# A graph layer by sorted windows: table copies issued by ScalarE at steps of the sort, and one chunk more in every turn

## The chip, the cores and the metric

The kernel runs on one core of a Trainium2 chip. The metric is the device time of one execution in microseconds, the median of several runs. The engines are named as in the profile: PE (TensorE products), PEld (its weight loads), DVE (VectorE), ACT (ScalarE), POOL (GpSimd) and SP (SyncE, which only issues transfers). A name with q, such as SPq, is the queue side of that engine.

## The reference

For 100,000 nodes of 64 features and 3,300,000 edges, sorted by target node, the layer normalises the features, applies a ReLU, sends the source row along every edge, averages over the edges of a target, and adds the result to the input:

```python
def _L0_gnn_ref(features, src, tgt, W, b):
    num_v = features.shape[0]
    local = features[tgt]
    nbr = features[src]
    x = jnp.concatenate([local, nbr - local], axis=-1)
    y = jnp.einsum('ec,oc->eo', x, W) + b
    s = jax.ops.segment_sum(y, tgt, num_segments=num_v)
    cnt = jax.ops.segment_sum(jnp.ones((y.shape[0],), y.dtype), tgt, num_segments=num_v)
    cnt = cnt[:, None]
    return jnp.where(cnt > 0, s / jnp.maximum(cnt, 1.0), 0.0)

h = jnp.maximum(_layernorm(x, axis=-1), 0.0)
x = x + _L0_gnn_ref(h, src, dst, L0_gnn_W, L0_gnn_b)
```

As the sum is linear, the kernel sums only the rows `h[src]` per target and counts them; the weights are applied once per node at the end.

## The kernel before

The program has five stages, which run one after another in time, with some overlap.

**Rows** (0 to about 440 us). For 28 groups of nodes the kernel normalises `x` and writes every row of `h`, split into three bf16 parts and a column of ones, to a DRAM tensor `h3` (named `h` in the profile; the write is L289, `h<-parts`). A row is 194 bf16 numbers, 388 bytes. It also writes `hb` from ACT's queue and clears the sums `acc`.

**The edges are divided** in two. 120 windows of 16,256 edges (`src_w`, `dst_w`) take the way of sorting; the rest, 377 chunks of 128 x 28 edges (`src_p`, `dst_p`), take the way of gathering.

**Chunks** (the generator `chunks`). For each of the 28 columns of a chunk POOL gathers 128 rows of `h` by an indirect transfer (L388, `nb<-h,si`, five buffers `nb`). DVE makes one-hot rows of the targets (L339, `hot`), PE multiplies them with the gathered rows (L393, `ps<-nb,hot`), DVE adds the three parts (L403, L405, `sums`), and POOL adds `sums` to `acc` by a transfer with accumulation (L365 in the first stages, L370 in the loop), issued 56 gathers after the sums. Index blocks `si` and `di` for 16 chunks are loaded by SP.

**Sort** (about 490 to 2750 us; the generator `sort_windows`). The target column `keys` is loaded (L418), the smallest target of every window found (L420, L422), sixteen pieces `s` of the source column are loaded (L434) and merged into the keys (L437 to L443), and then DVE and ACT run a sorting network. One exchange is an ACT copy `tmp` (L449) and DVE's minimum and maximum (L450, L451). After every step the generator yields its estimated nanoseconds. The caller spends them on gathers, `GATHER` nanoseconds for one:

```python
def gathers(ns):
    nonlocal owed
    owed += ns
    while owed > 0:
        next(ev, None)
        owed -= GATHER
```

At every second step from the 40th on the caller also writes one copy of 640 rows of `h` into the DRAM tensor `tables` (L891, 157 copies of 242.5 KB), in the layout in which the later stages load them. A scheduler then decides the order on each engine's queue: an instruction is placed as early as its priority and the modelled readiness of its inputs allow, unless `tc.issue_after(x)` sets it behind the instruction `x`. `last` holds, for each engine, the last instruction that others may be set behind.

**Filling of slots** (about 2750 to 3510 us; `fill_slots`). POOL fetches pieces of the sorted keys (322 gathers `kf<-ksort`, L692, and 120 gathers `kx<-ksort`, L663); DVE, ACT and PE turn them into index tables in DRAM.

**Pairs and turns** (`pairs`). For each pair of windows PE picks rows out of `tables` by one-hot products (L822, `gp<-tab,gh`), ACT moves them (L825, L826) and PE adds them by target (L836, `total<-gs,dh`). The first three pairs partly overlap the filling of slots; 57 more run in a loop of three turns of 19 pairs, with `KB` chunks of the gathering way in each turn. All chunks that are not in a turn are worked off ahead of the loop: `FIRST` and `KB` give their number, `PA`, as chunks in all minus three times `KB`. A closing stage (from about 16,205 us, L995 to L1015) applies the weights and writes the output.

Of the kernel before, what the change touches and what calls it, by code (L numbers as in the profile page):

```python
# [22 lines left out]
POOL = mybir.EngineType.Pool  # L23
SP = mybir.EngineType.SP
DVE = mybir.EngineType.DVE

P = 128
EPS = 1e-5
J = 28
CHUNK = P * J  # L30
SB = 19
KB = 102
U0 = 3
KG = 16
JH = 14
LAG = 3
GATHER = 1230
STEP = 1300
GAP = 8
JA = 16  # L40
# [2 lines left out]
CS = 640  # L43
NB = CS // P
# [15 lines left out]
TG = 3  # L60
# [3 lines left out]
def f32_of(bits):  # L64
    return float(np.array([bits], np.uint32).view(np.float32)[0])
# [12 lines left out]
def plan(v, e):  # L78
# [3 lines left out]
    turns = max(1, min((P // 2 - U0) // SB,  # L82
                       round((e - FIRST * CHUNK - 2 * U0 * ew) / (2 * SB * ew + KB * CHUNK))))
    nw = 2 * (U0 + turns * SB)
    chunks = -(-(e - nw * ew) // CHUNK)
    return wl, nw, max(chunks, turns * KB)


FIRST = 71


@with_exitstack
def gnn_preln(ctx: ExitStack, tc, x, src_w, dst_w, src_p, dst_p, src_a, dst_a, wT, b, out, V, E):
# [17 lines left out]
    nc = tc.nc  # L111
# [19 lines left out]
    NCH = src_p.shape[0]  # L131
    PA = NCH - (SETS - U0) // SB * KB
    NMT = -(-NCH // P)
# [9 lines left out]
    h3 = dram.tile([RT, CT], BF16, name="h3")  # L143
# [9 lines left out]
    tables = dram.tile([NTB, P, TG, NB * CT], BF16, name="tables")  # L153
# [157 lines left out]
    with tc.tile_pool(name="rows", bufs=5) as rows, \  # L311
# [3 lines left out]
        last = {}  # L315
# [5 lines left out]
        def behind():  # L321

            return tc.issue_after(last[DVE].ins) if DVE in last else nullcontext()

# [6 lines left out]
        def add_now(all_of_them=False):  # L331
            while later and (all_of_them or (later[0][0] <= count[0] and count[0] - count[1] >= GAP)):
                later.pop(0)[1]()
                count[1] = count[0]
# [76 lines left out]
        def drain(events):  # L411
            for _ in events:
                pass

        def sort_windows(keys, piece, small, ps):
# [5 lines left out]
            nc.vector.tensor_scalar_min(wb[:, 0:1], wb[:, 0:1], float(V - CH))  # L421
            last[DVE] = nc.vector.tensor_reduce(wb[:, 1:2], whole[:, :EW], axis=AX.X, op=ALU.max)  # L422
            yield 2 * EW
# [6 lines left out]
            for a in range(0, EW, PART):  # L430
# [11 lines left out]
                nc.vector.tensor_scalar(s[:, :n], s[:, :n], 10, BIAS | 1, op0=ALU.logical_shift_left, op1=ALU.bitwise_or)  # L442
                last[DVE] = nc.vector.scalar_tensor_tensor(d, d, 1, s[:, :n],  # L443
                                               op0=ALU.logical_shift_left, op1=ALU.bitwise_or)
# [1 line left out]
            nc.vector.memset(keys[:, EW:], f32_of(END))  # L446

            def exchange(lo, hi, tmp):
                nc.scalar.copy(tmp, lo)  # L449
                nc.vector.tensor_tensor(lo, tmp, hi, ALU.min)  # L450
                last[DVE] = nc.vector.tensor_tensor(hi, tmp, hi, ALU.max)  # L451

            def merge(p, k):
# [3 lines left out]
                def blocks(b, q, m):  # L457
                    r = keys[:, 2 * p * b:2 * p * (b + q)].rearrange("p (b l) -> p b l", l=2 * p)
                    if k < p:
                        r = r[:, :, k:2 * p - k]  # L460
                    r = r.rearrange("p b (m s t) -> p b m s t", s=2, t=k)
                    tmp = ps.tile([NW, PIECE], F32, name="tmp")
                    exchange(r[:, :, :, 0], r[:, :, :, 1],
                             tmp[:, :q * m * k].rearrange("p (b m t) -> p b m t", b=q, t=k))

                def run(a, n):
                    tmp = ps.tile([NW, PIECE], F32, name="tmp")
                    exchange(keys[:, a:a + n], keys[:, a + k:a + k + n], tmp[:, :n])

                def groups(a, n):  # L470
                    r = keys[:, a:a + 2 * k * n].rearrange("p (m s t) -> p m s t", s=2, t=k)
                    tmp = ps.tile([NW, PIECE], F32, name="tmp")
                    exchange(r[:, :, 0], r[:, :, 1], tmp[:, :n * k].rearrange("p (m t) -> p m t", t=k))
# [41 lines left out]
            def around(c):  # L515
                a = min(max(c // 2 * step + c % 2 * (step // 2) - H, 0), WL - L)
                return slice(a, a + L)

            def count_next():
                nonlocal nth  # L520
                nth += 1
                nc.scalar.activation(junk[:, 0], keys[:, around(nth)], AF.Sign, bias=bound[:, nth:nth + 1],
                                     scale=-GAIN, accum_out=pos[:, nth:nth + 1])

            p = 1
            while p < WL:
                k = p
# [37 lines left out]
            lo = piece.tile([NW, NHB + 2], F32, name="lo", bufs=1)  # L565
# [4 lines left out]
            for c in range(here + 1, NHB + 1):  # L570
                if nth < here:
                    count_next()
                last[DVE] = nc.vector.tensor_scalar(junk[:, 1], keys[:, around(c)], f32_of(BIAS + (c * CSH << 10)), None, op0=ALU.is_lt,
                                        op1=ALU.add, accum_out=pos[:, c:c + 1])
# [56 lines left out]
            slots[:] = at_i, first, row, fit, over, limit  # L631
            last.pop(DVE)

# [240 lines left out]
        with tc.tile_pool(name="few", bufs=1) as few:  # L874
            ev = chunks(0, PA)
            owed = 0.0
# [8 lines that stand above are left out]
            with tc.tile_pool(name="keys", bufs=1) as big, tc.tile_pool(name="piece", bufs=2) as piece, \  # L885
                    tc.tile_pool(name="sort_ps", bufs=2, space=PSUM) as ps:
                for i, ns in enumerate(sort_windows(big.tile([NW, WL], F32, name="keys"), piece, few, ps)):

                    k, r = divmod(i - 40, 2)
                    if 0 <= k < NCB and r == 0:  # L890
                        nc.sync.dma_start(tables[k // TG, :, k % TG].rearrange("p (b f) -> p b f", b=NB),  # L891
                                          h3[k * CS:(k + 1) * CS].rearrange("(b p) f -> p b f", b=NB))
                    gathers(ns)
            worst = few.tile([P, 1], F32, name="worst")
            nc.vector.tensor_reduce(worst, odd, axis=AX.X, op=ALU.max)
            with tc.tile_pool(name="w_ps", bufs=1, space=PSUM) as wps:
                w_ps = wps.tile([1, P], F32, name="w_ps")
                nc.tensor.transpose(w_ps, worst, ident)
                w_all = few.tile([1, 1], F32, name="w_all")
                nc.vector.tensor_reduce(w_all, w_ps, axis=AX.X, op=ALU.max)  # L900
                nc.vector.tensor_copy(turns[:, 0:1], w_all)
                nc.vector.tensor_scalar_mul(turns[:, 1:2], w_all, float(NF))

            with tc.tile_pool(name="load", bufs=3) as load, tc.tile_pool(name="hots", bufs=3) as hots, \
                    tc.tile_pool(name="g_ps", bufs=2, space=PSUM) as g_ps, \
                    tc.tile_pool(name="a_ps", bufs=1, space=PSUM) as a_ps:
                with tc.tile_pool(name="slots", bufs=2) as piece:
                    steps = pairs(0, U0, NE - AHEAD // 2)
                    for i, _ in enumerate(fill_slots(piece)):
                        for _ in range(SL // 2 if 2 < i < -(-NS // SL) else 0):  # L910
                            next(steps)
                for _ in steps:
                    gathers(2 * STEP)
                drain(ev)
                add_now(True)
                with tc.For_i(0, (SETS - U0) // SB, 1) as g:
                    ev = chunks(None, KB, PA + g * KB)
                    next(ev)
                    owed = 0.0
                    for _ in pairs(U0 + g * SB, SB):  # L920
                        owed += 2 * (KB * J - 1) / (SB * NE)
                        while owed > 0:
                            next(ev, None)
                            owed -= 1
                    drain(ev)
                    add_now(True)
# [126 lines left out]
```

## Time and profile before

| what | value |
|---|---|
| median of 3 runs | 16530.51 us (16521.81 to 16532.21) |
| the profiled execution, its own time | 16529.2 us |
| its span | 16527.4 us |
| PE busy | 13495.8 us (82%) |
| DVE busy | 13631.9 us (82%) |
| ACT busy | 10590.2 us (64%) |
| POOL busy | 11625.4 us (70%) |
| gathers L388 | 10556, mean 953 ns, 10059.1 us |
| table copies L891 | 157 issues, SP, 365.3 to 861.4 us |

The busy shares are averages over stages with different limits, so they say little by themselves. The timeline and the tables by stretches of time tell which engine is full in which stage. A wait is listed under the engine that waited, with what ended it. "Issue" is idle time that the profile cannot put down to anything. The durations of the program's own DMA issues on POOL are times of POOL, not of the transfer.

### The profile page before, as it was taken

Reading aid. Unit: us, or ns where it says so; the run is one execution under the profiler, and the core shown is the slowest. Engines: PE = TensorE matmul, PEld = TensorE weight load, DVE = VectorE, ACT = ScalarE, POOL = GpSimd, SP = SyncE. Lnnn points to the kernel's source line nnn. Section 1 sums busy time; section 2 is a strip of 40 time slices with the busy share of each in tenths; the row PEclk is TensorE's granted clock in tenths of the full one; section 3 lists DMA queues with packets and bytes.
Section 4 is the critical chain, followed back from the end, with each engine's and each line's share of the span. In section 5 each row is a group of like instructions: output and inputs, shape, how many; then the busy total and the mean of one; then the engine's idle time right before and its main releaser. Section 6 shows DMA issues by size and latency. Waiting matters only on the chain. (4 is left out here: it accounts for less than half of the span.)

```text
span 16527.4 us, 393944 instructions
## 1 busy us (share of the span) xinstructions
PE 13495.8 (82%) x149665; PEld 12959.6 (78%) x149665; DVE 13631.9 (82%) x14528; ACT 10590.2 (64%) x21095; POOL 11625.4 (70%) x11771
## 2 busy tenths in 40 slices
PE   6011110379999999999999999999999999999996
PEld 5011110369999999999899999999989999999996
DVE  6699996468888888888788888888878888888884
ACT  5144335466777777777677777777767777777772
POOL 4577777755777777777677777777767777777765
PEclk7555555689999999999999999999999999999998
DMA  8931112478999989999899999999879999999997
GB/s 295 152 50 39 39 39 63 139 221 255 279 281 280 279 279 279 281 279 278 253 280 279 280 279 279 278 281 278 278 249 279 281 282 280 279 280 279 279 276 282
DMA packets 1769028, 3974.67 MB, mean 240 GB/s; under 512 B 941660, under 2 KB 949607, under 8 KB 1759101
## 3 DMA queue, kind: packets, MB, share of 16 engines
q1 hardware_dynamic: 1289510, 3354.10, 61.8%
q0 software_dynamic: 473424, 569.44, 17.1%
q8 instruction: 1181, 19.35, 0.5%
q10 hardware_dynamic: 4176, 25.74, 0.4%
q14 instruction: 737, 6.04, 0.1%
HBM read 3750.40 MB, written 236.66 MB: 241 GB/s over the span
## 5 line engine op out<-in xcount | busy, mean ns | idle before, releaser
L388 POOL DMA_INDIRECT nb<-h,si x10556 | 10059.1, 953 | 3469.0 <-issue 3083.0
L836 PE MATMUL total<-gs,dh 128*128 128x193 bf16 x77280 | 8067.4, 247 | 65.2 <-ACT whole L844 29.1
L339 DVE TENSOR_TENSOR dh<-dt,c 128x2048 bf16<-128x2048 int16 x4860 | 5893.8, 1213 | 1718.9 <-PE total L836 1660.1
L836 PEld LDWEIGHTS <-dh 128*128 128x128 bf16 x77760 | 6725.8, 97 | 447.3 <-issue 85.1
L825 ACT CAST gs<-gp 64x386 bf16<-64x386 f32 x9420 | 4480.0, 476 | 3506.8 <-PE gp L822 3476.5
L822 PE MATMUL gp<-tab,gh 128*128 128x193 bf16 x56520 | 6356.8, 247 | 251.8 <-DVE gh L796 145.4
L822 PEld LDWEIGHTS <-gh 128*128 128x128 bf16 x58440 | 5092.8, 98 | 275.2 <-DVE gh L796 148.7
L796 DVE TENSOR_TENSOR gh<-srs,c 128x1536 bf16<-128x1536 int16 (+2 forms) x4920 | 4614.7, 939 | 29.1 <-PE gp L822 25.3
L826 ACT CAST gs<-gp 64x386 bf16<-64x386 f32 x9420 | 4494.5, 477 | 109.3
L393 PE MATMUL ps<-nb,hot 128*128 128x193 bf16 x10556 | 1805.6, 264 | 2131.1 <-DVE sums L405 1892.7
L393 PEld LDWEIGHTS <-hot 128*128 128x128 bf16 x10556 | 1044.7, 105 | 2196.3 <-DVE sums L405 1940.6
L449 ACT COPY tmp<-keys 120x1536 f32<-120x1536 f32 (+26 forms) x606 | 750.8, 1248 | 1352.5 <-DVE keys L451 1051.1
L450 DVE TENSOR_TENSOR keys<-tmp,keys 120x1536 f32<-120x1536 f32 (+26 forms) x606 | 867.3, 1466 | 71.2 <-ACT tmp L449 69.8
L451 DVE TENSOR_TENSOR keys<-tmp,keys 120x1536 f32<-120x1536 f32 (+26 forms) x606 | 869.0, 1464 | 1.3
L339 DVE TENSOR_TENSOR hot<-near,c 128x1792 bf16<-128x1792 int16 x754 | 814.2, 1080 | 0.1
L370 POOL DMA_DIRECT2D acc<-sums x306 | 305.9, 1000 | 287.4 <-DVE dh L339 102.4
L855 POOL DMA_DIRECT2D acc<-wsums x120 | 168.4, 1403 | 443.0 <-DVE wsums L851 150.5
L692 POOL DMA_INDIRECT kf<-ksort,at_i x322 | 330.3, 1026 | 110.2 <-issue 93.6
L697 DVE TENSOR_SCALAR sr<-kf 120x768 int32<-120x768 int32 (+1 forms) x27 | 15.3, 568 | 460.4 <-DMA kf<-ksort,at_i 443.5
L828 ACT CAST gs<-gp 128x386 bf16<-128x386 f32 x240 | 115.7, 482 | 203.2 <-PE gp L822 201.5
L1010 ACT COPY catT<-c_ps 128x512 f32<-128x512 f32 x112 | 56.2, 534 | 278.1 <-PE c_ps L1008 278.1
L726 PE MATMUL gp<-ident,df 120*128 120x120 f32 x161 | 30.5, 328 | 247.6 <-ACT df L718 222.5
(169 smaller groups left out, 4101.6 us busy)
## 6 DMA issues: line engine op xcount, KB each, us to landing
tab<-tables SPq DMA_DIRECT2D x3120, 727.5 KB
srs<-sr_d SPq DMA_DIRECT2D x1560, 384.0 KB
nb<-h,si POOLq DMA_INDIRECT x10556
tables<-h SPq DMA_DIRECT2D x157, 242.5 KB
h<-parts SPq DMA_DIRECT2D x28, 1358.0 KB
dt_d<-dt SPq DMA_DIRECT2D x26, 1440.0 KB
dt<-dt_d SPq DMA_DIRECT2D x1560, 24.0 KB
acc<-zeros SPq DMA_DIRECT2D x28, 910.0 KB
```

Of the source, the lines that this page charges most:

```text
L339: nc.vector.tensor_tensor(out.rearrange("p k (a d) -> p k a d", d=D), numbers[:, :, None].to_broadcast(shape), upto[:shape[0], :n].rearran ...
L388: last[POOL] = nc.gpsimd.indirect_dma_start(out=nb[:, j], out_offset=None, in_=h3, in_offset=bass.IndirectOffsetOnAxis(ap=si[:, u, j:j + 1 ...
L393: nc.tensor.matmul(ps, lhsT=before[1][:, j], rhs=before[2][:, j, :CE], start=j == 0, stop=j == J - 1)
L449: nc.scalar.copy(tmp, lo)
L450: nc.vector.tensor_tensor(lo, tmp, hi, ALU.min)
L451: last[DVE] = nc.vector.tensor_tensor(hi, tmp, hi, ALU.max)
L692: last[POOL] = nc.gpsimd.indirect_dma_start(out=kf[:, c, q], out_offset=None, in_=ksort, in_offset=bass.IndirectOffsetOnAxis(ap=at_i[:, c0 ...
L796: nc.vector.tensor_tensor(gh[:, a:z, :, :to].rearrange("p c i b s -> p (c i) b s"), srs[u, s // SL][:, c + a:c + z].rearrange("p c i s -> ...
L822: nc.tensor.matmul(gp[:, i], lhsT=ghots[t][:, i, b], rhs=of[:, :CE], start=b == 0, stop=b == len(parts) - 1)
L825: nc.scalar.copy(gs[t][:KS], gp[:KS])
L826: nc.scalar.copy(gs[t][KS:], gp[KS:, ::-1])
L836: nc.tensor.matmul(total[:, o, b % 2 * CE:b % 2 * CE + CE], lhsT=dhots[t][:, i, b * P:b * P + P], rhs=gs[t][:, i] if s < NS else beyond[u] ...
```

## The change

The copies into `tables` go from SP's queue to ACT's, and each is set behind the ACT copy `tmp` of its step, so that the scheduler cannot move it ahead. Gathers are paced at 1250 ns instead of 1230, every turn gets 103 chunks instead of 102, and `FIRST` goes from 71 to 68, which leaves 68 chunks instead of 71 ahead of the loop. From line 26 on, lines of the changed kernel stand one lower than before, and past L890 two lower.

```diff
+ACT = mybir.EngineType.Activation
...
-KB = 102
+KB = 103
...
-GATHER = 1230
+GATHER = 1250
...
-FIRST = 71
+FIRST = 68
...
             def exchange(lo, hi, tmp):
-                nc.scalar.copy(tmp, lo)
+                last[ACT] = nc.scalar.copy(tmp, lo)
                 nc.vector.tensor_tensor(lo, tmp, hi, ALU.min)
                 last[DVE] = nc.vector.tensor_tensor(hi, tmp, hi, ALU.max)
...
                     k, r = divmod(i - 40, 2)
                     if 0 <= k < NCB and r == 0:
-                        nc.sync.dma_start(tables[k // TG, :, k % TG].rearrange("p (b f) -> p b f", b=NB),
-                                          h3[k * CS:(k + 1) * CS].rearrange("(b p) f -> p b f", b=NB))
+                        with tc.issue_after(last[ACT].ins):
+                            nc.scalar.dma_start(tables[k // TG, :, k % TG].rearrange("p (b f) -> p b f", b=NB),
+                                                h3[k * CS:(k + 1) * CS].rearrange("(b p) f -> p b f", b=NB))
                     gathers(ns)
```

## The prediction

> **What bounds the kernel now.** I read the time in stages, because the page's chain of waits names only the last 1 to 2% (the closing stage, lines L998 to L1015), which the change does not touch. First the slices of the page:
>
> ```profile
> POOL 4577777755777777777677777777767777777765
> DMA  8931112478999989999899999999879999999997
> ```
>
> A slice is 413 us. DMA is busy in the first (rows) and from slice 8 on (turns), idle in the sort between; POOL never drops. The table by stretches shows which engine is full where (PE, PEld, DVE, ACT, POOL busy, clock, DMA share, GB/s):
>
> ```profile
> 600.00:800.00 200.00, 18.12 (x112) 15.45 (x112) 150.37 (x131) 39.12 (x25) 146.00 (x136) 0.53 1.18 149
> 1000.00:1200.00 200.00, 22.29 (x140) 19.49 (x140) 193.81 (x145) 80.37 (x61) 152.17 (x158) 0.53 0.20 41
> 3210.00:3310.00 100.00, 34.87 (x267) 31.47 (x266) 31.09 (x39) 35.34 (x74) 76.84 (x77) 0.65 0.38 119
> 3610.00:3710.00 100.00, 99.79 (x1148) 96.62 (x1146) 85.84 (x90) 72.56 (x153) 68.91 (x71) 1.00 0.88 278
> ```
>
> In the sort (line two) POOL shows 152 of 200 us, but the waits give each gather L388 another 0.30 us of "issue", so 158 instructions fill the 200 us: POOL is full. DVE at 194 is nearly full too. In the filling of slots (line three) only POOL is full. From 3610 on PE is full. The timeline shows that POOL goes from the last gather of the sort straight into the `kf` gathers, with no gap:
>
> ```profile
> 2909.49 0.94 POOL L388 DMA_INDIRECT nb<-h,si  x1 [0.30 <-issue]
> 2910.74 0.99 POOL L692 DMA_INDIRECT kf<-ksort,at_i  x1 [0.31 <-issue]
> ```
>
> DVE had finished its sort at about 2745 us and waits 179 us for these `kf`. So the path is: rows ready, first gather at 489.7, POOL without a pause until the last `kf` at 3510, then PE to 16190, then the closing stage. The start is disturbed. These are waits between 400 and 760 us (engine, line, whom for, total, times, longest) and the gathers' table (PE, POOL):
>
> ```profile
> DVE own L437 <- DMA s<-in_src_w: 85.4, 10, 38.6
> POOL nb L388 <- DMA si<-in_src_p: 48.4, 1, 48.4
> DVE wb L420 <- DMA keys<-in_dst_w: 46.2, 1, 46.2
> ...
> 489.00:880.00 391.00, 37.59 (x224) 264.95 (x255) 0.52 1.16 138
> 880.00:2880.00 2000.00, 227.71 (x1428) 1434.81 (x1514) 0.54 0.20 44
> ```
>
> The 157 table copies L891 leave SP from 365 to 861 us. While they last POOL gathers 255 rows in 391 us, afterwards 1514 in 2000. Subtracting additions L365 (1.626 + 0.30 = 1.93 us; 4 and 54 of them) leaves 1.50 against 1.25 us per gather.
>
> **What the Trainium skill says.** "DMA: Bandwidth & Descriptors", section "Issuing engines are not separate DMA queues": copies from any engine run on the same 16 DMA engines and interleave; another issuer saves only issue time. So moving to ScalarE frees no bandwidth; only the spreading can. This trace cannot test it: nearly nothing leaves ACT. The same page, section "Specifications", puts the smallest transfer for full rate at 512 B. The trace agrees: table rows are 388 B, and copies with gathers move 113 to 166 GB/s at a DMA share above 1.1, where the turns move 280 at 0.9.
>
> **The change, part by part.** I sum against the profiled run (16529.2 us, span 16527.4 plus 1.8); the median of the three runs is 1.3 higher.
>
> (a) Start of the gathers. The order on SP after the change has no copies between the last rows and `keys`. The `h<-parts` pairs left SP at 332.1, 359.9, 387.6, so every 27.8 us; the next, due at 415.4, left at 419.0 behind eight copies (17.68 us of SP). Last `h` therefore goes at about 419 instead of 421.8, last `hb` at 422 instead of 424.3. Landing took up to 9.6 us amid copies (387.64 to 397.24); I take 6, an estimate. `keys` waits for all these: it leaves at 428 instead of 441.6. Its transfer alone moved 195 GB/s (460 to 480 us), so 7.62 MB take 39 us and some 2 us of latency: landed at 469, `si` just behind, first gather at 470 instead of 489.7. **-20 us**; ends -6 (rows land no sooner) and -35 (`keys` at the 270 GB/s of the rows).
>
> (b) Gathers beside copies. 255 x 1.249 + 4 x 1.93 = 326 us against 391: 65 us lost. After the change one copy follows two steps of the sort, about 7 us (two exchanges of two 1.46 us DVE operations, plus one-hots). In the jam 112 copies took 543 to 861 us, 2.8 us each, so copies fill 40% and gathers 0.19 of the DMA engines: 0.6, no jam. In the turns, at 0.9, a gather takes 948 ns (142.21 us for 150 from 8200 to 8400), as in the quiet sort, and the 2856 of a turn wait for their forerunners only 12 us in all. I leave 15 of 65: **-50 us**. Ends: -65 (no loss left) and +11 (all 157 copies cost what the 135 of this stretch did, 0.48 us, so 76).
>
> (c) Pace and split. FIRST 71 to 68 and KB 102 to 103 keep 377 chunks: 68 before the turns instead of 71, 309 in them instead of 306. The instruction order shows 1764 gathers ahead of the first `kf` instead of 1792, and one addition fewer: 28 x 1.249 + 1.93 = **-37 us** on POOL's path (ends -35, -39). I give 1250 no other gain: POOL needs 1.249 plus 1.93/28, so 1.32 us per gather, either way.
>
> (d) PE later. With PE full, 1148 products took 99.79 us, 87 ns each, so a chunk costs 28 x 87 ns = 2.4 us (the 247 ns of the groups are latency). Three more in the turns, +7.3; between last `kf` and turns 10 chunks remain instead of 12, -4.9. **+2 us**; ends 0 and +10.
>
> (e) ScalarE. 157 issues at 0.62 us (two in 1.24 us on SP at 579.06) are 97 us over 314 steps. Behind each stands the next `tmp` copy L449 (after the change L450), for which DVE waits. ACT sits idle before L449 for 1051 us waiting on DVE, so I take 0. If the cover fails, DVE still has room: it starts 20 us earlier and loses the 87 us that it idled between 520 and 720 (113 busy of 200), so its sort ends near 2640 while `kf` starts near 2805. Ends: 0 and SP's median issue, 2.3 us x 157 = 361 us on ACT. A gain is excluded, as ACT gets only work added. SP loses those issues; its index and `s` loads move up. The DMA waits of the ACT copies are on transfers eight issues back, long landed.
>
> (f) POOL in the turns. One chunk more is about 36 us of POOL per turn of some 4065. I counted POOL's gathers minus PE's products in the second turn (from 8060 us): lead 47 after 100 us, 63 after 700, 97 after 2400, then capped by the five `nb` buffers. 28 gathers more over a turn slow that growth from 50 to about 36 per half turn; the lead stays positive. 0 us; ends 0 and +34 per turn.
>
> Sum: -20 - 50 - 37 + 2 = -105. 16529.2 - 105 = 16424, plus 1.3 for the median: 16425 us. `s` loads no longer wait, but that was DVE's time, not POOL's, and adds nothing.
>
> **Rivals.**
> 1. *The copies hinder as before, only spread.* For: POOL's own durations rose beside them (up to 2.7 us). Against: the share of 0.6. Then (b) is +11: -20 + 11 - 37 + 2 = -44, 16487.
> 2. *ScalarE becomes the stall, and it is slower.* Place: ACT's queue between `tmp` copies. If an issue blocks as SP's did (2.3 us), the sort steps slip. An addition is emitted 56 gathers (70 us) after its sums, so POOL absorbs about 70 us of DVE slip and then waits in full. It outweighs the 105 us from 175 us of slip on, 1.1 us per copy; at 2.3 us it gives 361 - 70 - 105 = +186, 16717. For: SP did block. Against: SP blocked behind a full queue, and its unblocked issue is 0.55 to 0.62 us.
> 3. *POOL becomes the bound in the turns.* +34 x 3 = 102 on top: 16527, no change. For: about 190 of 200 us are filled there. Against: the lead that I counted.
> 4. *The copies do not really spread.* Then (c) and (d) remain, -35: 16496. Against: the order shows each behind two `tmp` copies, the first after twelve.
>
> **Chances.** Forecast 0.74, rival 1 0.10, rival 2 0.09, rival 3 0.05, rival 4 0.02. About 0.2% (33 us, below 16497) is what a measurement here can tell from no change. Forecast, 1 and most of 4 are faster: 0.84; rival 3 and the rest of 4 the same, 0.06; rival 2 slower, 0.10. The ends of (a) to (d) without rivals give -139 to -30, 16391 to 16500; I widen down to 16375, since the rows' end may move more than I allow, and cut at 16495.
>
> **What would show it.** Right: first gather near 470; about 1.27 us per gather between 500 and 900; DMA share near 0.6 from 650 to 1800, 0.2 after; first `kf` near 2805, still straight behind a gather; turns unchanged within 5 us each. Wrong: `kf` waiting for DVE or ACT, POOL's additions waiting for `sums`, PE waiting for `nb` inside a turn, or issues of copies on ACT above 1.1 us.

## The result and the profile after

The changed kernel takes **16439.88 us** (median of five runs, 16428.62 to 16441.98), the kernel before took 16531.38 us beside it (median of five). The ratio is 0.9944 with a 95% interval of 0.9929 to 0.9958: 91.5 us less, where 105 were forecast. The profiled execution lasted 16428.62 us, 100.6 us less than the profiled one of before. It is the fastest of the five, 11.3 us under their median, so what is read from the two traces adds up to 100.6 and not to 91.5.

The slices of the page after the change:

```profile
POOL 4677777754777777777677777777767777777775
DMA  7434312488999999998799999999879999999997
```

DMA's 8 and 9 of the first two slices have become 7 and 4, and the fourth and fifth slice have risen from 1 to 4 and 3: the copies have moved out of the first 860 us. The groups of `tables` and the table by stretches (PE, PEld, DVE, ACT, POOL busy, clock, DMA share, GB/s) say where to:

```profile
L893 ACTq DMA_DIRECT2D tables<-h x157: 559/559/691, 686.1 to 1804.2; - x157
```

```profile
470.00:600.00 130.00, 13.28 (x84) 11.49 (x84) 128.70 (x106) 6.19 (x4) 102.63 (x90) 0.53 0.41 85
600.00:686.00 86.00, 13.19 (x56) 6.90 (x56) 82.39 (x65) 29.40 (x19) 66.19 (x66) 0.52 0.20 48
686.00:1804.00 1118.00, 124.55 (x756) 104.48 (x756) 965.93 (x738) 401.52 (x312) 851.11 (x876) 0.54 0.41 74
1804.00:2814.00 1010.00, 114.73 (x729) 99.84 (x729) 912.21 (x970) 499.32 (x641) 768.80 (x792) 0.53 0.22 49
3610.00:3710.00 100.00, 99.50 (x1146) 96.40 (x1144) 87.68 (x101) 71.07 (x150) 71.17 (x73) 1.00 0.88 271
```

The 157 copies leave ACT between 686 and 1804 us, at 0.56 us each. In that stretch DMA is busy to 0.41 and POOL issues 876 instructions, 846 gathers and 30 additions: 846 x 1.249 + 30 x 1.93 = 1114.6 of the 1118 us. Beside the spread copies the gathers lose 3 us in all. The share of DMA alone does not tell whether they lose: from 470 to 600 us, with no copy yet under way, it is 0.41 too, and there the 90 instructions are only 112 us of work in 130 us. With PE full (last line) nothing has changed. The timeline of POOL:

```profile
470.23 1.22 POOL L389 DMA_INDIRECT nb<-h,si  x1 [43.33 <-DMA si<-in_src_p]
...
2812.64 0.95 POOL L389 DMA_INDIRECT nb<-h,si  x1 [0.30 <-issue]
2813.89 0.98 POOL L693 DMA_INDIRECT kf<-ksort,at_i  x1 [0.31 <-issue]
```

The first gather starts 19.5 us earlier, the first `kf` 96.8 us earlier (2910.7 before), and still straight behind a gather. The last `kf` starts at 3404.7 instead of 3509.3, 104.6 earlier. The three turns last 4058.9, 4071.4 and 4072.8 us against 4056.2, 4068.2 and 4071.4, so some 2 us longer each.

Of these waits between 600 and 2900 us (engine, line, whom for; total, times, longest) the two of ACT for DMA were not there before, and the first, of DVE for ACT, came to 69.8 us then, the longest 2.3:

```profile
DVE keys L451 <- ACT tmp L450: 198.1, 79, 122.6
ACT tmp L450 <- DMA si<-in_src_p: 137.6, 2, 127.9
DVE sr L698 <- DMA kf<-ksort,at_i: 95.6, 4, 63.9
ACT tmp L450 <- DMA tables<-h: 67.2, 21, 3.5
```

ACT stood still for 127.9 us in the middle of the sort and DVE behind it for 122.6. DVE waits only 63.9 us for the first `kf` where it waited 179.0 before: the cover of the sort has shrunk to a third, but it held.

On two of the chips of the experiments all engines paused now and then, for tens of us, from about 690 us on, waiting for nothing that the program shows, and the kernel before took 27.1 to 27.3 ms there; runs from there are read only ahead of 690 us or one against another.

### The profile page after: what moved, and what is told of

The parts are those of the page before. It is cut to its first block, busy times and chain, and to the rows that moved or that the text cites. A ratio compares the mean times of both kernels' runs of the same rounds, so it can differ in the third digit from the quotient of the medians.

```text
span 16427.0 us, 393934 instructions
## 1 busy us (share of the span) xinstructions
PE 13503.9 (82%) x149665; PEld 12963.9 (79%) x149665; DVE 13621.6 (83%) x14528; ACT 10590.7 (64%) x21095; POOL 11621.9 (71%) x11771
## 5 line engine op out<-in xcount | busy, mean ns | idle before, releaser
L303 PEld LDWEIGHTS o_ps<-w_own,hT 128*128 128x128 f32 x784 | 155.1, 252 | 79.1 <-ACT hT L298 69.5
```

## The experiments

Every kernel was timed beside the kernel before on the same chip.

**The copies moved, pace and split old** (spread_only, spread_only_b), of the changed kernel:

```diff
-KB = 103
+KB = 102
-GATHER = 1250
+GATHER = 1230
-FIRST = 68
+FIRST = 71
```

> The changed kernel with the old pace and split (GATHER 1230, KB 102, FIRST 71): the copies alone are moved; 64 chunks of gathers stand ahead of the first `kf` as before the change. Theory (POOL's queue sets the first `kf`): the earlier start (-19.5 us) and the contention no longer met (-40 us) remain, the 28 gathers and the addition (-37 us) come back. First gather near 470, first `kf` near 2851, time -60 against before: about 16471 us, all of it ahead of the first `kf`. Rival A (the end of DVE's sort sets the first `kf`, the number of gathers does not): the whole gain stays, about 16440. Rival B (the split and pace carry it all): no gain, about 16531.

> The kernel of spread_only once more, because in its first run the engines paused for tens of us at a time all through the turns, and the kernel before took 27.2 ms there too. The copies alone are moved; pace and split stay old, 64 chunks of gathers ahead of the first `kf`. Theory (POOL's queue sets the first `kf`): -60 us against before, about 16471 us, first gather near 470, first `kf` near 2851 and straight behind a gather. Rival A (the end of DVE's sort sets it): the whole gain stays, about 16440. Rival B (split and pace carry it all): no gain, 16531.

The first run fell on a pausing chip: ratio 0.9987 (0.9980 to 0.9994) at 27220 us, first gather at 473.0. The second took 16464.57 us against 16524.76: ratio 0.9965 (0.9951 to 0.9978), **-60 us** as the theory had it. Its POOL:

```profile
2849.05 0.94 POOL L389 DMA_INDIRECT nb<-h,si  x1 [0.30 <-issue]
2850.30 0.99 POOL L693 DMA_INDIRECT kf<-ksort,at_i  x1 [0.31 <-issue]
```

2850.3 was expected at 2851. The 36.4 us that lie between this and the changed kernel's 2813.9 are one chunk of gathers. DVE's sort had stood still here too (133.6 us on ACT), so the end of the sort sets nothing: rival A is out, and so is B. No run spreads the copies from SP's queue, so whether spreading needs ACT as the issuer is not shown.

**Pace and split new, the copies as before** (split_only, split_only_b), of the kernel before:

```diff
-KB = 102
+KB = 103
-GATHER = 1230
+GATHER = 1250
-FIRST = 71
+FIRST = 68
```

> The kernel before with the new pace and split alone (GATHER 1250, KB 103, FIRST 68), its copies still leaving SP all at once; 63 chunks of gathers ahead of the first `kf`. Theory (POOL's queue sets it): one chunk fewer is 28 x 1.249 + 1.93 = 37 us less ahead of the first `kf`, one more per turn costs PE about 2 us in all: -35, about 16496 us, first `kf` near 2874, still straight behind a gather. Rival A (DVE's sort sets it): DVE is done at about 2745 and unchanged, so nothing is gained, 16531. Rival B (a chunk more in each turn makes POOL the bound there): +34 us in each of three turns, 16530 to 16600, with the turns longer than 4072 us.

> The kernel of split_only once more (the kernel before with GATHER 1250, KB 103, FIRST 68; its copies leave SP all at once), for the reason of spread_only_b; 63 chunks of gathers ahead of the first `kf`. Theory (POOL's queue sets it): 37 us fewer there, some 2 us more of PE in the turns: -35, about 16490 us on this chip, where before took 16525; with the -60 of spread_only_b that makes the whole change. First `kf` near 2874, still straight behind a gather. Rival A (DVE's sort sets it): nothing gained, 16525. Rival B (a chunk more in each turn makes POOL the bound there): 16525 to 16590, with turns longer than 4072 us.

On the pausing chip no difference could be told (1.0000, 0.9992 to 1.0009). The second run took 16535.58 against 16565.89 us: ratio 0.9980 (0.9973 to 0.9988), **-30 us**. `kf` is straight behind a gather again:

```profile
2898.64 0.95 POOL L388 DMA_INDIRECT nb<-h,si  x1 [0.30 <-issue]
2899.89 0.99 POOL L692 DMA_INDIRECT kf<-ksort,at_i  x1 [0.31 <-issue]
```

It comes at 2899.9 and not at 2874. The gathers started at 494.6 instead of 489.7, and 1764 x 1.249 + 57 x 1.93 = 2313 of the 2405 us up to `kf` are work: 92 us lost, where the profile of before lost 71. There is no profile of the kernel before on this chip, whose own time was 35 us longer too, so whether its jam was longer there stays open. The turns last 4060.0, 4072.3 and 4079.3 us, far from 34 us more in each (rival B). The two halves, -60 and -30, make the -91.5 of the whole: they add.

**Twice the copies** (copies_twice, copies_twice_b), of the changed kernel:

```diff
+    spare = dram.tile([NTB, P, TG, NB * CT], BF16, name="spare")
...
-                        with tc.issue_after(last[ACT].ins):
-                            nc.scalar.dma_start(tables[...
+                        for to in (tables, spare):
+                          with tc.issue_after(last[ACT].ins):
+                            nc.scalar.dma_start(to[...
```

> The changed kernel, but ScalarE issues each copy twice, the second into a spare table that nobody reads (extra work, same output). Theory (spread copies fit beside the gathers, the DMA engines have room): share of the DMA engines between 700 and 1800 us rises from about 0.42 to about 0.65, gathers keep 1.25 to 1.29 us each, and the loss is 0 to 15 us; ScalarE's second issue, 157 x 0.56 = 88 us, falls on DVE's sort, which ended near 2752 while the first `kf` is issued at 2814, so up to 26 us of it may show: 16440 to 16480 us. Rival A (each copy takes its price from the gathers, spread or not, 0.26 to 0.48 us as in the jam): another 40 to 76 us on POOL's path between 690 and 1800 us, 16480 to 16515, gathers there at 1.30 us or more. Rival B (issues on ScalarE stall the sort by more than they last): the additions of POOL wait for `sums` or `kf` for DVE, over 16500.

> The kernel of copies_twice once more, for the reason of spread_only_b: the changed kernel, but ScalarE issues each copy twice, the second into a spare table that nobody reads. The changed kernel is taken as 92 us under the kernel before. Theory (spread copies fit beside the gathers): DMA share between 700 and 1800 us from about 0.42 to about 0.66, gathers between 880 and 1804 us as many as in the changed kernel (699 and 25 additions), and 88 us more of issuing on ScalarE stay covered but for at most some 26 us: -66 to -92 against before. Rival A (each copy takes its price from the gathers, 0.26 to 0.48 us): 40 to 76 us more on POOL's path, about 32 to 58 gathers fewer by 1804 us, -16 to -52 against before. Rival B (issues on ScalarE stall the sort by more than they last): first `kf` no longer straight behind a gather, no gain over before or slower.

Both runs fell on pausing chips (27232.55 us, ratio 0.9990, 0.9983 to 0.9997; and 27091.84 us, 0.9988, 0.9982 to 0.9995), so the times don't decide. The stretch of the copies does, as the first run shared its chip with spread_only. The same stretch, in spread_only and then in copies_twice:

```profile
690.00:1804.00 1114.00, 108.59 (x672) 94.62 (x672) 840.44 (x621) 348.45 (x262) 766.07 (x787) 0.53 0.35 65
```

```profile
690.00:1804.00 1114.00, 104.13 (x644) 90.66 (x644) 826.50 (x608) 343.09 (x256) 767.82 (x787) 0.53 0.62 93
```

The share of DMA goes from 0.35 to 0.62, and POOL issues 787 instructions in both. The second chip gives 787 at 0.68. A price of 0.26 us per copy would have cost some 32 gathers. Spread copies take nothing from the gathers, and twice as many would not either (Rival A out). What the doubled issues do to the end of the sort on a chip without pauses isn't told.

**ACT as the issuer, all at once** (act_at_once, act_at_once_b), of the changed kernel:

```diff
-                        with tc.issue_after(last[ACT].ins):
-                            nc.scalar.dma_start(tables[...
+                        nc.scalar.dma_start(tables[...
```

> The changed kernel, but ScalarE issues the copies as soon as the rows are ready (no step of the sort to wait for); pace and split stay new. Theory (it is the spreading that helps, the issuer does not): the jam returns, +40 us between 490 and 900 us and 0 to 20 at the start of the gathers, so 16480 to 16500 us; besides ScalarE's issues should block behind full queues as SP's did (up to 2.3 us each, 361 us in all), the sort's first `tmp` copies come late, and if DVE's sort then ends beyond 2870 us it sets the first `kf` and up to 50 us come on top. Rival (the issuer is what helps: SP was blocked and its loads late, ScalarE's copies run beside the gathers for nothing): 16430 to 16450, as the changed kernel.

> The kernel of act_at_once once more, for the reason of spread_only_b: the changed kernel, but ScalarE issues the copies as soon as the rows are ready; pace and split stay new. In its first run the first gather came at 519.5 us, where the copies spread over the sort gave 473.0 and the copies leaving SP at once 491.7. Theory (the spreading helps, the issuer does not): the gathers start 49 us later than in the changed kernel and lose 40 us more in the jam, so first `kf` near 2900 and -35 + 28 = about 7 us under before, between -20 and +20; if ScalarE's blocked issues push the end of DVE's sort past 2900 us, up to 60 us more. Rival (the issuer is what helps): as the changed kernel, -92.

Ratio 1.0011 (1.0004 to 1.0017) in both runs, on pausing chips: 28 and 27 us slower than before, where the first expectation had 30 to 50 us faster, the second about 7, and the rival 92. The kernel it differs from by the issuer alone is split_only, and on the chip that the two shared it is 23 us slower. What comes ahead of the pauses fits this. The copies in the second run, and SP's queue:

```profile
L892 ACTq DMA_DIRECT2D tables<-h x157: 559/2573/40170, 372.9 to 907.1; - x157
```

```profile
436.56 0.36 SPq L419 DMA_DIRECT2D keys<-in_dst_w  x1
504.58 0.40 SPq L352 DMA_DIRECT2D si<-in_src_p  x1
```

ACT is blocked as SP was: median 2.57 us an issue, the longest 40 us. `keys` goes at 436.6, later than the changed kernel's 425.8, and `si` 68 us behind it, so the gathers start at 522.8 (519.5 in the first run). Table by stretches of the first run:

```profile
470.00:600.00 130.00, 8.84 (x28) 2.90 (x28) 49.14 (x22) 0.00 (x0) 52.36 (x51) 0.50 1.18 130
600.00:690.00 90.00, 4.71 (x28) 4.05 (x28) 49.71 (x51) 3.02 (x2) 66.31 (x62) 0.52 1.05 158
```

DMA is at 1.05 to 1.18, as with SP as the issuer, and POOL gets 113 instructions done by 690 us; spread_only got 156 done on the same chip, split_only 131. The issuer alone helps nothing; it even delays the start of the gathers by 28 us (519.5 against 491.7 in split_only). No wait of the views names what held SP between `keys` and `si`, but the semaphore events of the trace and the order of the program do. When a transfer lands it raises a completion semaphore, and the program gives `si` one that ACT's 17th copy uses before it. In the second run ACT sends that copy at 490.0 us, behind the issue of 40 us; it has landed at 504.5, and SP sends `si` at 504.6. In the first run the landing is at 501.2 and `si` at 501.3.

**The index blocks `si` loaded from ACT at their step** (si_act), of the changed kernel:

```diff
-                nc.sync.dma_start(si[:, :k], src_p[at]...
+                if dynamic is None and ACT in last:
+                    with tc.issue_after(last[ACT].ins):
+                        nc.scalar.dma_start(si[:, :k], src_p[at]...
+                else:
+                    nc.sync.dma_start(si[:, :k], src_p[at]...
```

> The changed kernel, but the blocks of gather indices `si` of the straight-line part are issued by ScalarE at the step of the sort, not by SP ahead of time. In the changed kernel one `tmp` copy of ScalarE waited 127.9 us, until 1078.6, for such an `si` load that SP could only issue when POOL had freed the block. Theory (POOL's queue sets the first `kf`, the stall is covered): that wait goes, DVE's sort ends some 110 us earlier and DVE then waits some 180 us for the first `kf` instead of 64, and the time stays within 6 us of the changed kernel's, so about -92 against before (near 16433 on this chip). Rival (the stall cost the path something: additions and `hot` of the gathers stand behind it on DVE): first `kf` 20 to 64 us earlier, about 16370 to 16415.

16457.89 against 16565.89 us, ratio 0.9936 (0.9922 to 0.9949): -108, not told apart from the changed kernel's 0.9944. The 127.9 us of ACT are gone. The end of DVE's sort, and its next instruction that waits for a `kf`:

```profile
2657.19 0.08 DVE L578 DVE_READ_ACCUMULATOR junk<-keys 120x1 f32 x1
2846.59 0.60 DVE L702 TENSOR_SCALAR sr<-kf 120x768 int32<-120x768 int32 x1 [175.46 <-DMA kf<-ksort,at_i]
```

The sort ends at 2657 instead of 2753, and all that comes of it is that DVE waits 175.5 us instead of 63.9. The stall was covered, as the theory says.

**Fewer gathers ahead of `kf`** (si_act_g1330, si_act_g1400): si_act with the pace alone changed.

```diff
-GATHER = 1250
+GATHER = 1330
```

> si_act with GATHER 1330: the order puts 59 chunks of gathers ahead of the first `kf` instead of 63, the four others behind it, between `kf` and the turns. Theory (POOL's queue sets the first `kf`, until DVE's sort end near 2640 does): four times 36.9 us, -148 against si_act, first `kf` near 2666, about 16285 us. Rival A (the room behind the first `kf` is full, so that POOL pays there for what it is spared ahead of it): as si_act, about 16433, the last `kf` or the start of the turns no earlier. Rival B (DVE's sort end stays near 2750 whatever the loads do): -62 at most, about 16370.

> si_act with GATHER 1400: 57 chunks ahead of the first `kf`. Theory: six times 36.9 us would be -221, but DVE's sort is done only near 2640, so `kf` waits for DVE from there on: -160 to -175 against si_act, about 16265 us, and the first `kf` no longer straight behind a gather. Rival A (room behind the first `kf` is full): no better than si_act or slower, over 16420. Rival B (the sort's end is set by POOL's gathers through additions and one-hots on DVE, which then go with them): the full -221, about 16212.

With 1330, 59 chunks ahead of the first `kf`: 16382.17 us, ratio 0.9889 (0.9874 to 0.9904), **-184 against before and -76 against si_act**, where -148 was expected. This is the fastest of the kernels tried. With 1400, 57 chunks: 16461.47 us, 0.9937 (0.9924 to 0.9951), no gain over si_act, where 160 to 175 us were expected. First `kf`: 2830.0, 2727.3 and 2749.5 us for 63, 59 and 57 chunks. What POOL waits for up to 2850 us, for 1330 and then for 1400:

```profile
POOL nb L393 <- DMA si<-in_src_p: 79.7, 2, 43.2
...
POOL acc L370 <- DVE sums L410: 11.9, 2, 11.6
```

```profile
POOL nb L393 <- DMA si<-in_src_p: 129.4, 4, 43.5
POOL acc L370 <- DVE sums L410: 66.0, 3, 36.0
```

One wait of 43 us for `si`, at the start, all have. Beyond it si_act had none, 1330 has 36.5 us and 1400 has 86: the block that ACT now loads only two chunks ahead comes late, and `sums` add to it. With 1330 the two come to 48 us, about the 45 that are missing at the first `kf` (148 - 103). A further 27 us go behind it, nearly all between the last `kf` and the first gather of the loop: 489.6 us in si_act, 513.0 with 1330. PE is busy for 470.0 and 481.5 of them, as the four chunks are now multiplied where PE is full, which the expectation had left out, and it stands for 20 and 32. With 1400 the room behind `kf` is full. The loop starts at 3915, 3839 and 3920 us in si_act, 1330 and 1400. The stretch ahead of it in the three:

```profile
3700.00:3850.00 150.00, 149.78 (x1720) 144.94 (x1718) 127.50 (x136) 108.78 (x229) 25.68 (x23) 1.00 0.82 250
```

```profile
3700.00:3850.00 150.00, 128.80 (x1441) 123.35 (x1439) 111.95 (x134) 84.65 (x179) 77.12 (x76) 0.93 0.72 214
```

```profile
3700.00:3850.00 150.00, 140.63 (x1598) 134.46 (x1596) 119.14 (x138) 92.59 (x195) 113.87 (x117) 0.99 0.82 246
3850.00:4000.00 150.00, 81.21 (x761) 67.24 (x760) 63.80 (x72) 47.62 (x100) 109.95 (x112) 0.70 0.49 144
```

In si_act POOL issues 23 instructions there and has time to spare; with 1400 it issues 117 and is full (117 x 0.30 us of issue on top of 114), gathers until 15 us before the loop, and PE, done with its pairs, stands for 69 of the 150 us of the last line: the gathers come too late for it (its `ps` waited 57.8 us for `nb` between 3320 and 4350 us, in 55 pieces). Between 59 and 57 chunks POOL's backlog moves from a place where it costs to another where it costs too.

**The blocks loaded earlier** (si_early_g1330): si_act_g1330, with each block loaded eight chunks ahead of its use.

```diff
-                if u == KG - 2 and q + 2 < n:
+                soon = KG - 2 if dynamic is not None else KG // 2
+                if u == soon and q + KG - u < n:
                     with behind():
-                        ahead = load(q + 2)
+                        ahead = load(q + KG - u)
```

> si_act_g1330 with each block of `si` (and its one-hot data) loaded eight chunks of gathers ahead of its use instead of two. There POOL waited 36.5 us for such a load and 12 us for `sums`, which is where 49 of the missing 148 - 99 us at the first `kf` went. Theory (the late load was the new wait): first `kf` near 2690 instead of 2727, DVE still waits some 80 us for it, everything behind is shifted by the same 36 us: -184 - 36 = about -220 against before. Rival A (the room behind `kf` is full, POOL arrives there with the same backlog whenever `kf` starts): the start of the turns does not move, -184. Rival B (loading earlier puts its DVE work ahead of the sort's): the sort ends later and takes the 36 us back, -184 or less, with DVE no longer waiting for `kf`.

On a pausing chip: 27073.15 us, ratio 0.9984 (0.9978 to 0.9991). The late load is gone; this is POOL's only wait for `si` up to 3300 us:

```profile
POOL nb L393 <- DMA si<-in_src_p: 43.3, 1, 43.3
```

The first `kf` starts at 2891.2, against 3053.4 in copies_twice_b on that chip, 162 us earlier for four chunks fewer, but the first gather of the loop comes at 4474.7 instead of 4487.7: 13 of the 162 us are left. That fits rival A, by which what is spared ahead of `kf` is paid behind it, but the pauses fall into this stretch, and copies_twice_b also issues each copy twice. si_act_g1330 was not timed on this chip, so whether this version beats it stays open.

## Why the prediction was right

**The path.** That POOL's queue sets the first `kf`, and nothing on DVE or ACT does, is shown from both sides: one chunk more or less ahead of it moves it by 36.4 us (spread_only_b against the changed kernel), and an end of the sort that comes 96 us earlier brings the first `kf` no earlier (si_act, at 2830.0). The runs compared here come from different chips; that the first `kf` stands straight behind a gather holds in each of them.

**(a) Start.** -20 forecast, -19.5 measured (first gather, before against after): `keys` left at 425.8 (428 forecast), landed at 468.6 (469), first gather at 470.2 (470).

**(b) Contention.** -50 forecast. Work of 2350 us took 2421 before and work of 2313 us took 2344 after, so the loss fell from 70.9 to 30.4: -40.5. The size was off in two ways that partly cancel. I left 15 us beside the copies, and 3 are left. But I had put all 65 us of the first 391 down to the copies, and between 470 and 686 us, ahead of the first copy, 21 us stay lost: there the `s` pieces of 480 KB are loaded from 513 to 606 us, and gathers beside them last up to 2.7 us instead of 0.95. No run leaves these loads out, so that they are the cause is argued from the time alone. My first rival, that spread copies hinder as before, is refuted; I had put the DMA share beside them at 0.6, it is 0.41: the 2.8 us per copy came from the jam, and spread a copy takes about (0.41 - 0.20) x 1118 / 157 = 1.5 us of the DMA engines, an estimate from the table by stretches. Twice as many copies, at 0.62 to 0.68, do no harm either. What the Trainium skill says in "DMA: Bandwidth & Descriptors", section "Issuing engines are not separate DMA queues", this case now bears out: ACT as the issuer without the spreading is no better, and the share stays above 1.0 (1.05 to 1.18 in act_at_once).

**(c) Split.** -37 forecast; 36.4 us between spread_only_b and the changed kernel at the first `kf`, and -30 (-45 to -20, by the interval) in the time of split_only_b.

**(d) PE later.** +2 forecast. Between the last `kf` and the turns 5.1 us are gained (4.9 forecast), and the three turns together grew by 7.3 us (7.3 forecast). The closing stage took 2 us more, so 4 us of the 104.6 at the last `kf` are gone by the end.

**(e) ScalarE.** 0 forecast, and 0 it is, but one sentence under it was **wrong**: that the waits of the copies are on transfers long landed. In this program the copies and loads take turns on eight completion semaphores, across SP and ACT, and a copy waits for the last user of its own. One had been given to the third `si` block, which SP could send only when POOL had gathered its first block. ACT's queue and SP's:

```profile
944.15 0.56 ACTq L893 DMA_DIRECT2D tables<-h  x1
947.86 2.82 ACT L450 COPY tmp<-keys 120x1536 f32<-120x1536 f32 x2 [3.23 <-DVE keys L452]
1077.95 0.56 ACTq L893 DMA_DIRECT2D tables<-h  x1
1078.55 1.44 ACT L450 COPY tmp<-keys 120x1536 f32<-120x1536 f32 x1 [127.87 <-DMA si<-in_src_p]
```

```profile
1074.41 0.39 SPq L352 DMA_DIRECT2D si<-in_src_p  x1
```

The next copy leaves 3.5 us after that load is sent, and the `tmp` copies queue behind it. So the sort ended at 2753 and not near 2640; si_act, where ACT sends that load itself at its step, gives 2657. Rival 2 (ACT stalls) had the right place with the wrong cause, and came to 138 + 67 us of waiting, of which none reached POOL; I put that down to the five `nb` buffers and the 56 gathers of grace, which no run varies. The price of one issue, 0.56 us against the 0.62 that I took, was nearly right. That the stall cost nothing was luck in part: the cover was reckoned for another kind of stall, and 63.9 us of it were left.

**(f) POOL in the turns.** 0 forecast. Counted alike in both profiles, POOL's lead over PE in the second turn is 47, 62 and 84 gathers before after 100, 700 and 2400 us, and 47, 56 and 76 after. (My 97 for the last does not come out again; some records of products are missing.) It grows more slowly and stays positive; rival 3 is out. Rival 4 is out by the 686 to 1804 us of the copies.

The first three terms, -19.5 - 40.5 - 37 = -97, are what the first `kf` gained. From there to the last `kf` another 7.8 us were gained (598.6 us before, 590.8 after), for which the prediction had no term; in the other profiles from chips without pauses this stretch lasts 594.1 to 598.7 us, and why it was shortest here I do not know. With the +4 behind it the sum is -101, beside 100.6 between the two profiled executions, where -105 was forecast. That close fit is luck in part, as these 7.8 us nearly make up for the 9.5 that (b) fell short; by the medians, -91.5, the forecast was 13.5 us too high.

## What to carry to other kernels

Before moving work off a busy moment, find the queue that sets the next stage and count in its own instructions what the moment costs; then spread, and do not expect anything from a new issuer alone. An engine off that path may stall for a tenth of a millisecond unseen, so look for the cover that is left as well as for the time. And a balance of work across a stage border (chunks ahead of `kf` or behind it) has a best point that runs must find: 63, 59 and 57 chunks gave -108, -184 and -104.

## What the runs showed of the hardware that I had not expected

- A transfer on one queue can wait for a load that another queue has not yet been able to send, through a completion semaphore that the program gave to both: ACT stood for 127.9 us behind a load of SP, and with all copies on ACT's queue at once a load of SP stood for 65 to 68 us behind a copy of ACT.
- Gathers of 388-byte rows ran at full pace beside copies at DMA shares of 0.41 to 0.68, and lost 0.25 us each at 1.16, beside copies and `s` pieces (65 us over 255 gathers, before the change). The share is no measure by itself: from 470 to 600 us in the changed kernel, with `s` pieces loaded and no copy, they lost 18 us in 130 at a share of 0.41.
- 157 copies put on ACT's queue at once blocked it for up to 40.2 us in one issue.
